# A graph network's second stage: other planned durations for its transfers, and one batch's attention put behind the last scores

## The chip, the cores and the metric

The kernel runs on one core of a Trainium2 chip, as one launch. The metric is the device time of that launch in microseconds. Three timed runs of the kernel before gave 3127.03, 3133.86 and 3125.08 us; their median, 3127.03 us, is what the changed kernel is compared with.

## The reference

Four graph layers follow each other on `x` (128 graphs of 128 nodes with 128 features, f32) and an adjacency `adj` (128 x 128 per graph, int32). Each layer adds its result to `x`. The change lies in the attention of the first one, whose core is this (`h` is the normalised, rectified `x`):

```python
D = jnp.abs(h[:, :, None, :] - h[:, None, :, :])        # 128 graphs, 128 x 128 pairs, 128 features
p = jnp.einsum('bijc,oc->bijo', D, W1) + b1             # 64 values per pair
p = (p - mean(p)) / jnp.sqrt(var(p) + EPS) * g1 + be1   # mean and variance over all graphs and pairs
s = jnp.einsum('bijo,uo->biju', leaky(p), W2)[..., 0] + b2[0]
A = softmax(jnp.where(adj > 0, s, NEG))
y = jnp.einsum('bij,bjc->bic', A, h) @ Wg.T + bg        # then normalised over all graphs
```

Two normalisations go over all 128 graphs. So all pair values have to exist before the first score, and all `y` before the second layer.

## The kernel before

The two normalisations cut the kernel into three stages. The first (to about 1253 us) makes the pair values of every graph. They are symmetric, so only half of them is kept: a tile `v` of 128 x 4064 f32 (2032 KB) per graph. Eight graphs' tiles stay in SBUF, those of the other 120 go to HBM (`pairs_d`). The second stage reads them back, makes scores, attention and `y`. The third runs everything else, four graphs at a time, and starts when `y` has been normalised.

The second stage takes the graphs in 16 batches of eight (`GS`). The batch that stayed in SBUF, number 15, comes first, then 0 to 14. So batch 14 is the last, and 13 the last but one. Its steps:

- `graph_scores` (L668 on): loads `v` of one graph (L677, on SP's DMA queue, into one of eight buffers); two halves of it get scale and bias on ACT (L657) and the leaky part on DVE (L428, at the end of `leaky`), the rest a rectifier on ACT (L664, tile `r`); then PE multiplies all with the weights (L702). The eight graphs of a batch gather in one PSUM tile `sc`. One graph's matmuls are called a score, or score group, below. When PE has finished a graph, its `v` buffer is free for the next load.
- `score_table`: after the eighth score, DVE adds a bias to the table (L721, tile `us`: the table step). Then POOL's DMA queue writes it to HBM in four pieces with the rows skewed (L731), and, when they have landed, reads it back (L742, tile `u`) in the layout that the symmetric matrix needs. Two tables in HBM are used in turn.
- `edges`, per four graphs: loads `adj` (L753, POOL's queue), makes the mask `negm` on DVE (L757) and squares the edges on ACT (L774) for the kernel's choice of third stage; loads `h` (L761, SP's queue, tile `ht`) and multiplies it with `Wg` (L765, tile `pz`, copied to `zg` at L768).
- `attention`, per four graphs, so twice per batch: an add on POOL (L784) completes `u`; PE sums the upper half, the transposed lower half and the mask (L791 to L794, tile `pl`: the logits); maximum and difference on DVE (L799, L801), exponential on ACT (L803), sum and division on DVE (L806 to L809), transposes on PE (L813), a copy on ACT (L816), the product with `zg` on PE (L820, tile `py`), the bias on ACT (L823), the store of `y` on POOL's queue (L825), and its statistics on DVE (L830, L831).
- `y_norm` takes the statistics of all graphs and gives scale and bias (`y_sc`, `y_bi`) to the third stage. `edge_types` (L849 to L857) makes the flag on which the program branches into the third stage.

The order of all this is not written out by hand. A planner, `in_order`, runs while the program is built. Each step is a generator that yields `(engine, planned duration, buffers taken, buffers freed)` before it emits its instructions. The planner starts up to ten chains at a time, gives each step a begin from when its engine, its predecessor and its buffers are free, and emits the step that can begin first; among equals, the older chain. `"wait", t` delays a chain in the plan by `t` us; `"after", name` holds a step until the plan has seen `"done", name`. Planned durations emit nothing. They only decide the order in which instructions stand on the engines, and each engine runs its instructions in that order. What really holds an instruction back on the chip are semaphores, which follow from the data and the buffers.

Of the kernel before, what the change touches and what calls it, by code (L numbers as in the profile page):

```python
# [24 lines left out]
GS = 8  # L25
GB = 4
# [20 lines left out]
PE, ACT, DVE, POOL, DMA = "PE", "ACT", "DVE", "POOL", "DMA"  # L47
# [115 lines left out]
def kernel(ctx: ExitStack, tc: tile.TileContext, x, adj, w, out):  # L163
    nc = tc.nc
    NB = x.shape[0]
# [267 lines left out]
    with tc.tile_pool(name="h_pool", bufs=1) as h_pool, tc.tile_pool(name="pairs", bufs=B_V) as b_v:  # L433
# [193 lines left out]
        with tc.tile_pool(name="b2", bufs=2) as b2p, tc.tile_pool(name="b_s", bufs=2, space=PSUM) as b_s, tc.tile_pool(  # L627
            name="b_ps", bufs=6, space=PSUM
        ) as b_ps:
            scores, masks = {}, {}  # L630
# [24 lines left out]
            def leaky_part(part, n):  # L655
                yield ACT, 0.2 + 0.00092 * n, "", ""
                nc.scalar.activation(part, part, AF.Identity, bias=h_bi, scale=h_sc)  # L657
                yield DVE, 0.15 + 0.00105 * n, "", ""
                leaky(nc.vector, part, part, 0.01)

            def relu_part(part, n, made):
                yield ACT, 1.1, "r", ""
                made["r"] = b2p.tile([P, 1024], F32, tag="r", name="r", bufs=B_R)
                nc.scalar.activation(  # L664
                    made["r"][:, 0:n], part, AF.Relu, bias=h_bi, scale=h_sc
                )

            def graph_scores(order, i):  # L668


                b = order[i]
                if b in here:
                    v = here.pop(b)
                else:
                    yield DMA, 5.2, "v", ""
                    v = b_v.tile([P, NPAIR], F32, tag="v", name="v")
                    nc.sync.dma_start(v, pairs_d[b])  # L677
                    yield "done", ("loaded", b)
                lin, made = first[NQ - 1], {}
                for a, e in ((0, lin // 2), (lin // 2, lin)):  # L680
                    yield "fork", leaky_part(v[:, a:e], e - a)
                yield "fork", relu_part(v[:, lin:NPAIR], NPAIR - lin, made)
                yield "join",
                r = made["r"]
                if i:
                    yield "after", ("w2", order[i - 1])
                yield PE, 3.2, "" if i else "sc", "v r"
                if i == 0:
                    scores[b // GS] = b_s.tile([P, 512], F32, tag="sc", name="sc")
                sc = scores[b // GS]  # L690
                for t in range(2):
                    k = b % GS + 2 * GS * t
                    begins, ends = i == t == 0, i == GS - 1 and t == 1
                    for q in [*range(NQ), NQ]:
                        rows = slice(QR * min(q, NQ - 1), QR * min(q, NQ - 1) + QR)
                        n = 8 * width[min(q, NQ - 1)]
                        if q < NQ:
                            z = v[:, first[q] + t * n : first[q] + t * n + n]
                        else:
                            z = r[:, t * n : t * n + n]  # L700
                        wz = w_slide if q < NQ - 1 else w_line if q < NQ else w_relu
                        nc.tensor.matmul(  # L702
                            sc[rows, 0:n], wz[:, 31 - k : 63 - k], z,
                            start=begins and q < NQ, stop=ends and q != NQ - 1,
                            tile_position=(0, rows.start),
                        )
                yield "done", ("w2", b)
                if i == GS - 1:
                    yield "done", ("scores", b // GS)

            def score_table(k):

                yield "after", ("scores", k)
                yield DVE, 1.6, "us", "sc"
                sc = scores.pop(k)
                sd = scores_d[k % 2]
                us = b2p.tile([P, 512], F32, tag="us", name="us")
                for s in range(2):
                    n = 8 * width[2 * s]
                    half = slice(64 * s, 64 * s + 64)  # L720
                    nc.vector.tensor_scalar(  # L721
                        us[half, 0:n], sc[half, 0:n], b2_rows[half, :], None, ALU.add
                    )
                yield POOL, 2.6, "u u", ""
                u = b2p.tile([P, GS, W], F32, tag="u", name="u")
                for q in range(NQ):
                    skewed = bass.AP(
                        tensor=sd.tensor, offset=sd.offset + QR * q * ROW + 1,
                        ap=[[W + 1, QR], [4 * ROW, 8], [1, width[q]]],
                    )  # L730
                    nc.gpsimd.dma_start(  # L731
                        skewed,
                        us[QR * q : QR * q + QR, 0 : 8 * width[q]].rearrange(
                            "p (r j) -> p r j", r=8
                        ),
                    )
                yield "wait", 3.0
                yield POOL, 1.2, "", "us"
                by_row = bass.AP(
                    tensor=sd.tensor, offset=sd.offset, ap=[[ROW - 1, P], [W + 1, GS], [1, W]]  # L740
                )
                nc.gpsimd.dma_start(u, by_row)  # L742
                yield "wait", 8.0
                for g in range(GS // GB):
                    yield "fork", attention(k * GS // GB + g, u[:, g * GB : g * GB + GB, :])
                yield "join",

            def edges(g):

                b0 = g * GB  # L750
                yield POOL, 0.7, "adj", ""
                adjs = b2p.tile([P, GB, P], I32, tag="adj", name="adj")
                nc.gpsimd.dma_start(adjs, adj_t[:, b0 : b0 + GB, :])  # L753
                yield "wait", 3.0
                yield DVE, 0.8, "negm", ""
                negm = b2p.tile([P, GB, P], F32, tag="negm", name="negm")
                nc.vector.tensor_scalar(negm, adjs, 0, NEG, ALU.is_le, ALU.mult)  # L757
                yield "fork", of_types(g, adjs)
                yield DMA, 0.6, "ht", ""
                ht = b2p.tile([P, GB, P], F32, tag="ht", name="ht")  # L760
                nc.sync.dma_start(ht, h_d[g])  # L761
                yield PE, 1.0, "pb", "ht"
                pz = b_ps.tile([P, GB, P], F32, tag="pb", name="pz")
                for i in range(GB):
                    nc.tensor.matmul(pz[:, i, :], ht[:, i, :], wgT, start=True, stop=True)  # L765
                yield ACT, 0.65, "zg", "pb"
                zg = b2p.tile([P, GB, P], F32, tag="zg", name="zg")
                nc.scalar.copy(zg, pz)  # L768
                masks[g] = negm, zg
                yield "done", ("edges", g)  # L770

            def of_types(g, adjs):
                yield ACT, 0.65, "", "adj"
                nc.scalar.activation(  # L774
                    adjs.bitcast(F32), adjs, AF.Square, bias=nhalf[:, 0:1], accum_out=squares[:, g : g + 1]
                )
                to_see.remove(g)
                if not to_see:
                    yield "done", "types"

            def attention(g, u):
                flat = "p g j -> p (g j)"
                yield POOL, 0.6, "", ""
                nc.gpsimd.tensor_tensor(  # L784
                    u[:, :, 0 : W - P], u[:, :, 0 : W - P], u[:, :, P:W], ALU.add
# [86 lines left out]
            ]  # L872
            makers = []

            for k in [NB // GS - 1, *range(NB // GS - 1)]:
                of_edges = [partial(edges, k * GS // GB + g) for g in range(GS // GB)]
                order = sorted(range(GS * k, GS * k + GS), key=lambda b: b not in here)
                of_graphs = [partial(graph_scores, order, i) for i in range(GS)]

                n = 0 if makers else 2  # L880
                makers += of_graphs[:n] + of_edges + of_graphs[n:] + [partial(score_table, k)]
# [484 lines left out]
def program(arrays):  # L1366

    import concourse.bacc as bacc

    nc = bacc.Bacc("TRN2", target_bir_lowering=False, num_devices=1)  # L1370
    ins, aps = {}, {}
    for name in ["x", "adj"] + _WEIGHTS:
        a = arrays[name]
        ins[f"in_{name}"] = a
        aps[name] = nc.dram_tensor(
            f"in_{name}", a.shape, mybir.dt.from_np(a.dtype), kind="ExternalInput"
        ).ap()
    out = nc.dram_tensor("out_0", arrays["x"].shape, F32, kind="ExternalOutput").ap()
    with tile.TileContext(nc) as tc:
        kernel(tc, aps["x"], aps["adj"], aps, out)  # L1380
    return nc, ins
# [10 lines left out]
```

## Time and profile before

| | us |
|---|---|
| median of three runs | 3127.03 |
| profiled execution, its own time | 3131.72 |
| its span, first to last instruction | 3129.9 |
| first score work of the second stage on ACT | 1253.3 |
| table step of batch 13 (DVE) | 1978.6 |
| table step of batch 14, the last | 2014.6 |
| last logits begin on PE | 2030.8 |
| `y_bi` done, third stage begins | 2052.0 |

The profile is one execution on the chip. "Busy" counts the time in which an engine has an instruction in work. A line of a timeline gives start and duration, then the engine, the source line, what is written from what, and in brackets how long the engine had been idle before and what ended that. The chain of waits follows the work that ended last back from the end: at each step to what released it, or else to the instruction ahead of it on its engine.

Shares of the whole span mix three stages with different limits. Over the span PE is busy 91%, DVE 85%, ACT 84%, POOL 48%. In the second stage, from 1400 to 1900 us, PE is busy 83 to 87 us of each 100, DVE 73 to 78, ACT 78 to 84, and the DMA engines move 383 to 407 GB/s.

These are the DMA issues of the second stage on the page (count, size of each, median time from issue to landing); the 240 of `v` are 120 stores of the first stage and 120 loads of the second:

```profile
v<-v SPq DMA_DIRECT2D x240, 2032.0 KB, 8.9
...
ht<-h SPq DMA_DIRECT2D x64, 256.0 KB, 6.3
u<-s POOLq DMA_DIRECT2D x16, 768.0 KB, 11.7
...
adj<-in_adj POOLq DMA_DIRECT2D x32, 256.0 KB, 7.5
y<-yt POOLq DMA_DIRECT2D x32, 256.0 KB, 6.2
```

### The profile page before, as it was taken

The numbers are of one execution on the slowest core, as the hardware profiler recorded it, in microseconds if no ns is written. First come the engines' busy times: TensorE is split into PE (matmuls) and PEld (weight loads), VectorE is DVE, ScalarE is ACT, GpSimd is POOL, SyncE is SP. The second block draws the span as 40 slices with busy tenths as digits, with TensorE's granted clock in tenths as the row PEclk, the third lists the DMA queues.
The fourth block names the chain that finished last, engine by engine and source line by source line (L and its number), as shares of the span: only waits on it lengthen the run. The fifth ranks groups of instructions, "written<-read, shape, count | busy, mean of one in ns | idle before, by whom it ended". The sixth has DMA issues, their size and how long they took to land. (4 is left out here: it accounts for less than half of the span.)

```text
span 3129.9 us, 47376 instructions
## 1 busy us (share of the span) xinstructions
PE 2852.8 (91%) x17526; PEld 1588.3 (51%) x17577; DVE 2656.4 (85%) x4730; ACT 2626.3 (84%) x3050; POOL 1494.6 (48%) x953
## 2 busy tenths in 40 slices
PE   6999999999999999787988888879999999999997
PEld 2444434333443333233333333367877777787776
DVE  6999999999999999776877877667787787787886
ACT  4999999999999998887877878657777877787786
POOL 5999999999999997111111111121222222222202
PEclk8999999999999999898999999989999999999999
DMA  3555555555555651899999999620111111111000
GB/s 120 241 239 240 242 239 244 227 227 244 236 227 228 252 224 41 351 393 381 402 405 406 397 409 400 227 75 11 45 48 35 48 38 45 41 38 42 18 1 22
DMA packets 150722, 606.53 MB, mean 194 GB/s; under 512 B 15633, under 2 KB 99026, under 8 KB 119762
## 3 DMA queue, kind: packets, MB, share of 16 engines
q1 hardware_dynamic: 140242, 569.86, 46.0%
q0 software_dynamic: 10240, 33.53, 3.0%
q8 instruction: 143, 2.34, 0.3%
q14 instruction: 97, 0.79, 0.1%
HBM read 322.74 MB, written 280.61 MB: 193 GB/s over the span
## 5 line engine op out<-in xcount | busy, mean ns | idle before, releaser
L552 POOL TENSOR_TENSOR d<-he 128x2016 f32<-128x2016 f32 (+1 forms) x288 | 1021.6, 3573 | 68.1 <-PE ph L569 62.2
L569 PE MATMUL ph<-d,w1T 128*64 128x512 f32 (+1 forms) x4096 | 927.5, 595 | 36.5 <-DVE d L549 17.6
L555 ACT ACTIVATE d<-d 128x2016 f32<-128x2016 f32 (+1 forms) x352 | 675.0, 1921 | 13.1 <-POOL d L552 13.0
L584 DVE BATCH_NORM_STATS2 six<-v 128x6 f32<-128x512 f32 (+1 forms) x1024 | 624.6, 670 | 5.6 <-ACT v L579 5.4
L569 PEld LDWEIGHTS ph<-d,w1T 128*64 128x64 f32 x4096 | 308.0, 136 | 546.2 <-issue 397.3
L579 ACT COPY v<-ph 128x1008 f32<-128x1008 f32 (+1 forms) x512 | 509.6, 1028 | 30.7 <-PE ph L569 27.9
L549 DVE TENSOR_TENSOR d<-he,pt 128x2048 f32<-128x2048 f32 (+1 forms) x224 | 505.5, 2257 | 2.6 <-PE ph L569 2.3
L939 POOL TENSOR_TENSOR rs<-ve,nhalf 128x4 f32<-128x4 f32 x96 | 119.1, 1241 | 738.6 <-DVE ve L936 480.4
L428 DVE SCALAR_TENSOR_TENSOR v<-v 128x1528 f32<-128x1528 f32 x256 | 434.0, 1742 | 34.2 <-ACT v L657 33.5
L657 ACT ACTIVATE v<-v,h_bi,h_sc 128x1528 f32<-128x1528 f32 x256 | 413.2, 1664 | 6.7 <-DVE h_bi L420 6.7
L702 PE MATMUL sc<-v,w_slide 128*32 128x512 f32 (+1 forms) x1536 | 322.6, 601 | 17.2 <-DVE v L428 16.9
L1095 PE MATMUL pa<-vals,p 128*128 128x99 f32 (+2 forms) x2048 | 253.2, 279 | 11.3 <-DVE p L966 7.7
L1095 PEld LDWEIGHTS pa<-vals,p 128*128 128x128 f32 x2048 | 248.5, 197 | 29.1 <-DVE p L966 11.3
L702 PE MATMUL sc<-v,w_line 128*32 128x504 f32 x512 | 261.0, 592 | 0.0
L702 PE MATMUL sc<-r,w_relu 128*32 128x504 f32 x512 | 259.1, 588 | 0.0
L966 DVE SCALAR_TENSOR_TENSOR p<-p,q 128x1024 f32<-128x1024 f32 (+1 forms) x192 | 206.7, 1083 | 48.5 <-ACT q L1082 24.4
L569 PE MATMUL ph<-both,us 128*64 128x512 bf16 x1920 | 236.4, 379 | 0.0
L569 PEld LDWEIGHTS <-us 128*64 128x64 bf16 x1920 | 124.4, 110 | 147.5 <-issue 91.6
L1081 ACT ACTIVATE p<-z 128x1024 f32<-128x1024 f32 x128 | 133.2, 1041 | 35.2 <-PE z L962 34.8
L664 ACT ACTIVATE r<-v,h_bi,h_sc 128x1008 f32<-128x1008 f32 x128 | 157.6, 1231 | 0.0
L702 PEld LDWEIGHTS sc<-v,w_slide 128*32 128x32 f32 x1536 | 65.1, 109 | 160.1 <-DVE v L428 83.3
L803 ACT ACTIVATE e<-e 128x512 f32<-128x512 f32 x32 | 20.2, 631 | 141.0 <-DVE e L801 141.0
(255 smaller groups left out, 4505.4 us busy)
## 6 DMA issues: line engine op xcount, KB each, us to landing
v<-v SPq DMA_DIRECT2D x240, 2032.0 KB, 8.9
xg<-in_x SPq DMA_DIRECT2D x64, 256.0 KB, 3.0
ht<-h SPq DMA_DIRECT2D x64, 256.0 KB, 6.3
u<-s POOLq DMA_DIRECT2D x16, 768.0 KB, 11.7
h<-he SPq DMA_DIRECT2D x32, 256.0 KB, 2.6
adj<-in_adj SPq DMA_DIRECT2D x32, 256.0 KB, 2.9
adj<-in_adj POOLq DMA_DIRECT2D x32, 256.0 KB, 7.5
y<-yt POOLq DMA_DIRECT2D x32, 256.0 KB, 6.2
```

The costliest lines, as they stand in the source:

```text
L428: engine.scalar_tensor_tensor(out, v, slope, v, ALU.mult, ALU.max)
L549: nc.vector.tensor_tensor(dv, later, own, ALU.max if larger else ALU.subtract)
L552: nc.gpsimd.tensor_tensor(dv, later, own, ALU.subtract)
L555: nc.scalar.activation(d[:, 0 : 4 * n], d[:, 0 : 4 * n], AF.Abs)
L569: nc.tensor.matmul(ph[64 * a : 64 * a + 64, t, 0:n], wt, x_, start=part == 0, stop=not larger or part == 3,)
L579: nc.scalar.copy(v.rearrange("p (t e) -> p t e", t=2), ph[:, :, 0:n])
L584: nc.vector.bn_stats(made["six"][:, 2 * q + t, :], v[:, t * n : t * n + n])
L657: nc.scalar.activation(part, part, AF.Identity, bias=h_bi, scale=h_sc)
L664: nc.scalar.activation(made["r"][:, 0:n], part, AF.Relu, bias=h_bi, scale=h_sc)
L702: nc.tensor.matmul(sc[rows, 0:n], wz[:, 31 - k : 63 - k], z, start=begins and q < NQ, stop=ends and q != NQ - 1, tile_position=(0, rows.st ...
L966: nc.vector.scalar_tensor_tensor(p, p, FLOOR, q, ALU.max, ALU.max)
L1095: nc.tensor.matmul(pa_all[:, h * (DH + 1) : h * (DH + 1) + n], p[:, h, :], vals_all[:, e : e + n], start=True, stop=True,)
```

## The change

Three planned durations get longer: the load of `v` from 5.2 to 5.8 us, the landing of the table's writes from 3.0 to 5.0, and the landing of `adj` from 3.0 to 8.0. None of them emits an instruction.

The order of the batches gets a name, `batches`, and `attention` is told its batch `k`. For the last batch but one (13), the planner holds the whole attention, from its add on POOL on, until it has planned the last score of the last batch (14). No instruction is added or taken away, and no tile or buffer changes.

```diff
-                    yield DMA, 5.2, "v", ""
+                    yield DMA, 5.8, "v", ""
...
-                yield "wait", 3.0
+                yield "wait", 5.0
                 yield POOL, 1.2, "", "us"
...
-                    yield "fork", attention(k * GS // GB + g, u[:, g * GB : g * GB + GB, :])
+                    yield "fork", attention(k, k * GS // GB + g, u[:, g * GB : g * GB + GB, :])
...
                 nc.gpsimd.dma_start(adjs, adj_t[:, b0 : b0 + GB, :])
-                yield "wait", 3.0
+                yield "wait", 8.0
                 yield DVE, 0.8, "negm", ""
...
-            def attention(g, u):
+            def attention(k, g, u):
                 flat = "p g j -> p (g j)"
+                if k in batches[-2:-1]:
+
+                    yield "after", ("scores", batches[-1])
                 yield POOL, 0.6, "", ""
...
-            for k in [NB // GS - 1, *range(NB // GS - 1)]:
+            batches = [NB // GS - 1, *range(NB // GS - 1)]
+            for k in batches:
```

## The prediction

> **What bounds the kernel now.** I read the slices of the page first. They show three stretches; the change touches only the middle one (about 1253 to 2052 us), where PE, ACT and DVE are all near 80% and the transfers near 100%. So I asked next for the windows of that stretch, then for who waits for whom in it, then for the chain through one batch of eight graphs, and last for the DMA queue of POOL.
>
> The slices of PE and DMA (40 of 78.2 us), one window of the stretch (columns: busy time and count of PE, PEld, DVE, ACT, POOL; TensorE clock; share of the DMA engines; GB/s), and the waits from 1340 to 1950 us:
>
> ```profile
> PE   6999999999999999787988888879999999999997
> ...
> DMA  3555555555555651899999999620111111111000
> ```
>
> ```profile
> 1600.00:1700.00 100.00, 85.89 (x476) 35.23 (x472) 77.65 (x84) 83.22 (x76) 14.52 (x22) 0.93 1.01 404
> ```
>
> ```profile
> POOL u L784 <- DMA u<-s: 130.7, 12, 13.5
> ACT e L803 <- DVE e L801: 106.4, 24, 11.9
> DVE mx L799 <- PE pl L794: 105.4, 24, 11.3
> PE pl L791 <- POOL u L784: 75.6, 12, 10.1
> ```
>
> The reader is to see that the DMA share is full, and yet that no line has an engine waiting for a load of `v`: PE, then DVE, then ACT all wait for `u`, the score table that comes back from HBM, once a batch. POOL's timeline through one batch and then the chain of waits (start, us, what) say what a batch's period is made of:
>
> ```profile
> 1833.86 2.36 POOL L731 DMA_DIRECT2D s<-us  x4 [7.52 <-DVE us L721]
> 1844.93 0.89 POOL L742 DMA_DIRECT2D u<-s  x1 [8.71 <-PE sc L702]
> 1856.11 1.40 POOL L784 TENSOR_TENSOR u<-u 128x256 f32<-128x256 f32 x2 [10.29 <-DMA u<-s]
> ...
> 1881.48 2.33 POOL L731 DMA_DIRECT2D s<-us  x4 [7.52 <-DVE us L721]
> ```
>
> ```profile
> 1856.88 2.08 PE pl L791 x2
> ...
> 1864.35 0.70 DVE mx L799
> ...
> 1868.98 0.63 PE pt L813 x4
> ...
> 1872.28 3.52 PE sc L702 x16
> ...
> 1876.89 3.53 PE sc L702 x20
> ```
>
> Period: 1881.48 - 1833.86 = 47.6 us. The table's DVE step starts 1.0 before its first write, at 1832.8, and the next one at 1880.4. From there to the logits (`pl`) at 1856.9 it is 24.1 us of two transfers in series (write 11.1, read 11.2); from the logits to the last score of the batch 23.5 us of PE work in its order. Their sum is the period. The read stands between "five score groups of the next batch" and "three score groups and the rest of the attention" in PE's order: what PE has in front of the logits is free while it fits into 24.1 us (it waited 5.3 at the end), what PE has behind them is paid in full.
>
> **What the Trainium skill says.** "DMA: Bandwidth & Descriptors", section "Queues, rings and completion order": each DMA engine takes turns between the queues that have work for it. The trace agrees: `u`, on POOL's queue, took 11.2 us here beside loads on SP's, and 5.4 (issued at 1989.6, its add at 1995.1) when none was left. So the two transfers shrink only when SP's queue is empty during them. "TensorE: Matmul & The Clock Gate", section "What's actually happening": an idle PE falls to half clock. It agrees: the first two `pl` matmuls took 2.08 us after the wait, the same pair of the second group 1.02. "Perfetto Trace Analysis", section "What "DMA-bound" means", looks for the bound in the DMA engines; here a share of 1.01 stands beside compute that never waits for them, so I follow the waits.
>
> **The change part by part.** Constants (5.2 to 5.8, 3.0 to 5.0, 3.0 to 8.0), the list `batches` and the argument `k` emit nothing; they decide the order. So I read the order of the two programs engine by engine. In before, every batch from the third attention on has on PE: 5 score groups, 2 logits, 1 score, 2 transposes, py, pz, py, score, pz, score. In after there are three patterns in turn, from the fourth attention on (four times A, four times B, three times C):
> A: 4 scores, logits, 2 scores, transpose, pz, py, transpose, score, py, pz, score.
> B: 4 scores, logits, score, 2 transposes, py, pz, py, 2 scores, pz, score.
> C: 5 scores, logits, score, transpose, pz, py, score, transpose, pz, py, score.
> The slower loads of the plan (5.8) let it think that four graphs fill the transfers. On the chip the loads are ahead, four groups take some 17 us (DVE does a half graph in 1.69: eight in 13.48), and PE waits sooner. The wait costs nothing new, but a score group (3.5) goes from the free side to the paid one.
>
> Walk from the logits, durations as above (logits 7.4 for the pair with half a clock, transpose 0.6, py 0.9, pz 1.1):
> A, PE: 7.4 + 3.5 + 3.5 + 0.6 + 1.1 + 0.9 + 0.6 + 3.5 + 0.9 + 1.1 + 3.5 = 26.6, with ACT's copies just inside it; I take 26.8, which is +3.3 on 23.5.
> B, DVE: second maximum at 7.5, its two steps 1.4, two sums 3.0, mask 0.35, two statistics 2.15, and eight half graphs before the table step, 13.5: 27.9, later than PE's 27.1; +4.3.
> C, PE: behind its second transpose stands ACT's copy at 19.9 (ACT does three half graphs, 1.6 each, and its other steps ahead of it), then py 0.9 and a score 3.5: 24.3, +0.8.
> The second and third attention move as C does, from 22.8 and 24.2: +1.6 together.
> Sum: 4 x 3.3 + 4 x 4.3 + 3 x 0.8 + 1.6 = 34.4 us. Do the 24.1 us shrink? Loads are issued as scores end. One score fewer stands before the wait, so SP's queue empties some 5 us sooner, at about 33 us after the table step instead of 38, still after `u` has landed at 23. I take no gain; bounds per batch are -2 (a quarter of the way to the 16.5 from the table step at 1978.6 to the add at 1995.1, when the loads ended) and +2: in A and C the store of `y`, on POOL's queue, is issued about 2 us before the table's writes instead of 7.5, and lies ahead of them.
>
> SP: one load of `ht` stands one place earlier among the loads of `v`; its buffer is free by then: 0. POOL: both loads of `adj` stand before both stores of `y`; the table's writes stay behind these: 0, else the +2 above.
>
> The moved attention (batch 13: 2 adds on POOL, 24 matmuls of logits, transposes and py and their loads, 2 x 5 steps of DVE, 2 x 3 of ACT, 2 stores). Before, it and two pz stood among the last eight scores: table step of batch 13 at 1978.6, of batch 14 at 2014.6, 36.0 us. After, the eight scores stand alone and ACT sets their pace: 6.5 graphs to do x 4.23 = 27.5, then 1.7 on DVE and 2.3 to 2.6 on PE: 31.5, a gain of 4.5. Then the moved work fills the wait for the last table. By the new order, from the last table step: logits to 5.7, pz 6.8, transpose 7.4, py 9.8, second transpose 11.0, py 12.8, its bias on ACT 13.5, its store 14.1; the last `u` took from 2014.6 to 2030.8 until its logits ran, 16.1. POOL's last add stands behind both stores, so the cover has 2 us left; without it each us of delay is a us of the end. Two things are late next: the flag for the branch is made some 7 us later (third-stage loads go out at about 10 us instead of 3; they are wanted at 37), which keeps them out of the way of `u`; and PE comes warm to the last logits. 37.3 us from table step to `y_bi` become about 35.2. Tail: -4.5 - 2.1 = -6.6.
>
> Sum against the profiled execution (3131.7 us, span 3129.9): +34.4 - 6.6 = +27.8, so about 3159.5; from the median of 3127.0, 4.7 lower: **3155 us**.
>
> **The rivals.** A run of this kernel is told from no change by about 0.3%, 9.4 us.
> 1. Forecast: the score moved behind the logits is paid. 0.64.
> 2. The transfers set the period: 47.7 us x 404 GB/s are 19.3 MB, and eight loads, the table and three small arrays sum to about that. Then `u` comes back sooner as the queue runs dry, the 34 us vanish and the tail remains: 3127 - 6.6 = 3120. For it: the share of 1.01. Against: no wait for a load; and at the early wait of 10.1 us, until 1376, the queue ran dry (171 GB/s from 1384 to 1388) only after `u` had landed. 0.17.
> 3. The change does what its constants say: PE's wait goes. Steady batches can't go below their transfers, so only the first ones (51.8, 50.9, 49.0) come down to 47.7, about -8, with the tail: 3112. Against: four scores before the logits, not six. 0.04.
> 4. As 1, with the stores of `y` delaying the table by 2 us in seven batches: +14, 3169 to 3172. It decides where a store is still running when the writes start. 0.15.
> Slower is then 0.64 + 0.15 = 0.79; rival 2 falls to 0.12 within and 0.05 below; faster 0.05 + 0.04 = 0.09. Range 3120 to 3176: the lower half of 2, and 3, are left out (about 0.12), and the top of 4 (0.07). The forecast's own range, by ±1.2 us a batch: 3140 to 3170.
>
> **What would show it.** Right: POOL's table writes about 51 us apart in A and B and 48.5 in C, PE waiting 8 to 10 us before the logits in A and B, transfers at 24 us, DMA share down to about 0.95, the last eight scores 31 to 32 us long. Wrong: a period of 47.7 with shorter transfers (rival 2), or logits that don't wait.

## The result, and the profile after

The changed kernel takes 3178.88 us (median of 4 runs, 3176.96 to 3190.89) against 3128.23 for the kernel before (4 runs, 3125.08 to 3133.86). The ratio is 1.0164, with a 95% interval of 1.0145 to 1.0182. It is slower, as forecast, but by 50.7 us and not by 28; 3178.9 lies above the range of 3120 to 3176. The profiled execution took 3179.55 us, its span 3177.8.

The slices of the page again (40 of 79.4 us), then one window of the second stage with the same columns as before the change:

```profile
PE   6999999999999998878787878879999999999997
...
DMA  3655655555555541999999999640111111111000
```

```profile
1600.00:1700.00 100.00, 75.42 (x401) 30.50 (x400) 66.05 (x72) 71.58 (x66) 13.27 (x20) 0.88 0.88 344
```

Every engine does less per 100 us, the DMA engines too: their share was 1.01 and is 0.88, at 344 GB/s instead of 404. Nothing became busier, so something is waited for longer. The waits from 1380 to 1990 us name it (total, times, longest):

```profile
POOL u L787 <- DMA u<-s: 146.5, 11, 13.7
DVE mx L802 <- PE pl L797: 143.8, 14, 13.3
ACT e L806 <- DVE e L804: 143.0, 14, 13.9
...
PE pl L794 <- POOL u L787: 106.9, 11, 11.3
```

It is the same wait as before, for the table `u` on its way back from HBM, but PE's part of it is now 9.7 us a time instead of 6.3. (All lines from the change on have moved by 3 to 4.) POOL's timeline through one batch of pattern A shows the period and the read:

```profile
1765.63 2.34 POOL L731 DMA_DIRECT2D s<-us  x4 [2.81 <-DVE us L721]
1776.07 0.90 POOL L742 DMA_DIRECT2D u<-s  x1 [8.09 <-PE sc L702]
1790.52 1.40 POOL L787 TENSOR_TENSOR u<-u 128x256 f32<-128x256 f32 x2 [13.55 <-DMA u<-s]
...
1816.16 0.56 POOL L828 DMA_DIRECT2D y<-yt  x1 [5.20 <-ACT yt L826]
1819.25 2.35 POOL L731 DMA_DIRECT2D s<-us  x4 [2.53 <-DVE us L721]
```

The period is 1819.25 - 1765.63 = 53.6 us; the forecast was about 51. From the issue of the read to the add on its result pass 1790.52 - 1776.07 = 14.5 us, where it was 11.2. The writes ahead of it, from the first write to the issue of the read, took 10.4 here and 11.1 before.

From the table step (DVE, L721), the first write (L731), the issue of the read (L742), its add (L787), the first logits (L794) and the next table step I summed the eleven middle batches, those from the fourth table step to that of batch 13:

| us, 11 batches | before | after | difference |
|---|---|---|---|
| first write to issue of the read | 125.1 | 117.6 | -7.5 |
| issue of the read to its add | 125.5 | 156.2 | +30.7 |
| table step to logits: these two, the step itself and the add | 270.6 | 293.9 | +23.3 |
| logits to the next table step | 258.4 | 297.1 | +38.7 |
| sum of the periods | 528.9 | 590.9 | +62.0 |

Ahead of these, the fourth table step comes at 1443.6 instead of 1449.7 (-6.1). Behind them, from the table step of batch 13 to `y_bi`, it is 67.0 us instead of 73.4 (-6.4). 62.0 - 6.1 - 6.4 = 49.5, and the spans differ by 47.9.

So the paid score cost 38.7 where 32.8 was forecast, and the way from table step to logits cost 23.3 where nothing was: the read 30.7 more, the writes ahead of it 7.5 less. What stood opposite the read can be seen on SP's queue. SP's timeline around one table step of before (at 1832.8), and then of after (at 1604.2):

```profile
1832.02 3.70 SPq L677 DMA_DIRECT2D v<-v  x2
1835.77 0.47 SPq L761 DMA_DIRECT2D ht<-h  x1
1840.65 0.32 SPq L677 DMA_DIRECT2D v<-v  x1
1841.02 0.44 SPq L761 DMA_DIRECT2D ht<-h  x1
1844.03 39.30 SPq L677 DMA_DIRECT2D v<-v  x7
```

```profile
1603.42 0.32 SPq L677 DMA_DIRECT2D v<-v  x1
1603.79 0.77 SPq L761 DMA_DIRECT2D ht<-h  x1
1606.81 0.32 SPq L677 DMA_DIRECT2D v<-v  x1
1607.17 0.54 SPq L761 DMA_DIRECT2D ht<-h  x1
1612.06 45.33 SPq L677 DMA_DIRECT2D v<-v  x7
```

In before, the two loads of `ht` go out 2.9 and 8.2 us after the table step, in after 0.4 before and 2.9 after it: about one load of `v` earlier. In the order of SP's queue both stand one load of `v` earlier in every middle batch. The DMA view of the stretch in which the data of one read is moved, first packet to last, of before (1849.2 to 1855.2) and of after (1780.2 to 1788.5), shows what that does (q1 is SP's queue, q0 POOL's; packets, MB, share of the 16 engines):

```profile
q1 hardware_dynamic: 229, 1.55, 65.5%
q0 software_dynamic: 188, 0.78, 35.5%
```

```profile
q1 hardware_dynamic: 198, 2.64, 79.3%
q0 software_dynamic: 174, 0.77, 23.3%
```

The same 0.77 MB of `u` came with 1.55 MB of SP's loads in 6.0 us before, and with 2.64 MB in 8.3 us after. In the trace's packet records a packet of `v` has 16,256 bytes and takes some 630 to 650 ns in the mean, one of `ht` 2,048 bytes and 90 to 100 ns, one of `u` mostly 4,608 bytes and 185 to 200. Per engine, ten of `u` stood in before beside 5.0 of `v` and 7.5 of `ht` (5.0 x 0.63 + 7.5 x 0.10 + 10 x 0.2 = 5.9 us), in after beside 10.1 of `v` and 0.9 of `ht` (10.1 x 0.65 + 0.9 x 0.09 + 10 x 0.19 = 8.5). In the mean of the eleven reads the 4.2 us from the issue to the first packet did not change; the data took 6.5 us before and 8.8 after, and 0.5 more passed between the last packet and the add. That is the reading; the experiments test it.

### The profile page after: what moved, and what is told of

The parts are those of the page before. It is cut to its first block, busy times and chain, and to the rows that moved or that the text cites. A ratio compares the mean times of both kernels' runs of the same rounds, so it can differ in the third digit from the quotient of the medians.

```text
span 3177.8 us, 47365 instructions
## 1 busy us (share of the span) xinstructions
PE 2853.8 (90%) x17526; PEld 1585.2 (50%) x17577; DVE 2658.3 (84%) x4730; ACT 2625.1 (83%) x3050; POOL 1495.3 (47%) x953
## 5 line engine op out<-in xcount | busy, mean ns | idle before, releaser
L428 DVE SCALAR_TENSOR_TENSOR v<-v 128x1528 f32<-128x1528 f32 x256 | 436.7, 1744 | 48.0 <-ACT v L657 46.6
L1099 PEld LDWEIGHTS pa<-vals,p 128*128 128x128 f32 x2048 | 247.8, 196 | 28.3 <-DVE p L970 11.2
L802 DVE TENSOR_REDUCE mx<-pl 128x4 f32<-128x512 f32 x32 | 22.0, 688 | 180.8 <-PE pl L797 180.8
L794 PE MATMUL pl<-u,ident 128*128 128x512 f32 x64 | 48.8, 855 | 133.0 <-POOL u L787 133.0
```

Of the source, the lines that this page charges most:

```text
L428: engine.scalar_tensor_tensor(out, v, slope, v, ALU.mult, ALU.max)
L1099: nc.tensor.matmul(pa_all[:, h * (DH + 1) : h * (DH + 1) + n], p[:, h, :], vals_all[:, e : e + n], start=True, stop=True,)
```

## The experiments

Each ratio is that of the experiment to the kernel before, with its 95% interval. The sums over eleven middle batches are made as above.

**One: the changed kernel, with `ht` put back by one load.** The issue of `ht` is held until the load of one more `v` has been issued, or until its reader comes; the order on the compute engines stays.

```diff
                     nc.sync.dma_start(v, pairs_d[b])
+                    to_load.discard(b)
+                    issue_held()
...
-                nc.sync.dma_start(ht, h_d[g])
+                held.append((ht, h_d[g]))
+                if not to_load:
+                    issue_held()
...
```

> The changed kernel, with each load of ht issued one place later on SP's queue, behind the next load of v, where the kernel before has it; the order on PE, ACT, DVE and POOL is that of the changed kernel. Theory P (place of ht): the read of u grew from about 11.4 to 14.2 us because POOL's queue and SP's take turns packet by packet, and only large packets of v stand opposite u when both ht are through; then the read is back at 11 to 12 us, from table step to logits it is 24 to 25 us instead of 26.6, and the kernel takes about 3179 - 11 x 2.3 = 3154 us (3148 to 3162). Theory R (the read is longer because fewer loads stand behind it, whatever the place of ht): read 14 us, 3179 us.

Measured: 3154.25 us (3142.50 to 3159.95), 1.0084 (1.0059 to 1.0110). The eleven reads sum to 125.5 us, as in before (after: 156.2), table step to logits to 268.2 (after: 293.9), logits to table step to 293.0 (after: 297.1). POOL's timeline of one batch of pattern A:

```profile
1600.35 2.34 POOL L739 DMA_DIRECT2D s<-us  x4 [2.81 <-DVE us L729]
1611.45 0.90 POOL L750 DMA_DIRECT2D u<-s  x1 [8.75 <-PE sc L704]
1621.91 1.40 POOL L798 TENSOR_TENSOR u<-u 128x256 f32<-128x256 f32 x2 [9.57 <-DMA u<-s]
...
1650.24 2.35 POOL L739 DMA_DIRECT2D s<-us  x4 [2.53 <-DVE us L729]
```

The read takes 10.5 us and the period is 49.9, with four scores ahead of the logits all the same. So about half of the loss, 24.6 us of 50.7 by the medians, is the place of `ht`. Without it the time is near the 3155 forecast, in part by luck: the walks behind the logits still cost 34.6, but the fourth table step came 4.9 us earlier than before, where 1.6 later was forecast, and the end saved 3.6 instead of 6.6.

**Two: the kernel before, with `ht` one load earlier.** The load of `v` is held instead, until the next `v` or `ht` is issued or its first reader comes.

```diff
-                    nc.sync.dma_start(v, pairs_d[b])
+                    issue_held()
+                    held.append((v, pairs_d[b]))
...
                 nc.sync.dma_start(ht, h_d[g])
+                issue_held()
...
```

> The kernel before, with each load of ht issued one place earlier on SP's queue, in front of the load of v that it followed, where the changed kernel has it; all else in the order of before. Theory P: read of u 13.5 to 14.5 us instead of 11.4, table step to logits 26 to 27 us, logits to the next table step unchanged at 23.5, so a batch takes about 50 us and the kernel 3128 + 12 x 2.3 = 3156 us (3148 to 3164). Theory R: nothing moves, 3128 us.

Measured: 3160.01 us (3158.34 to 3164.53), 1.0111 (1.0081 to 1.0140). Reads 158.5, table step to logits 295.5, logits to table step 266.7 (before: 258.4). One batch:

```profile
1649.08 2.33 POOL L742 DMA_DIRECT2D s<-us  x4 [7.52 <-DVE us L732]
1660.16 0.89 POOL L753 DMA_DIRECT2D u<-s  x1 [8.74 <-PE sc L707]
1674.31 1.40 POOL L796 TENSOR_TENSOR u<-u 128x256 f32<-128x256 f32 x2 [13.27 <-DMA u<-s]
...
1700.48 2.33 POOL L742 DMA_DIRECT2D s<-us  x4 [6.97 <-DVE us L732]
```

The read takes 14.2 us where PE's order has not been touched, and where POOL is idle for about 7 us before the table's writes, as in before. It is the place of `ht` alone; the stores, rival 4 of the prediction, have no part in it. I had expected the walk behind the logits to stay at 23.5 us; it took 24.2 in the mean. PE's two groups of logits took 8.1 us there and 7.35 in before, and that is the whole of the 8.3 us by which 266.7 exceeds 258.4. Why they are slower was not taken apart: in experiment four they took 7.9, after waits no longer than those of before.

**Three and four: the durations apart.** Three is the kernel before with only the 5.8; four is the changed kernel with 5.2 again, so with the two waits and the moved attention.

```diff
-                    yield DMA, 5.2, "v", ""
+                    yield DMA, 5.8, "v", ""
```

> The kernel before with one planned duration changed, the load of v from 5.2 to 5.8 us. PE then has four score groups ahead of the logits in every batch from the third attention on, and both loads of ht two places earlier. Theory A (one score group behind the logits is paid, and ht is through before the read): logits to table step 26.6 to 27.5 us, table step to logits 26 to 27, a batch about 53.5, the kernel 3128 + 12 x (3.1 + 2.3) = 3193 us (3183 to 3203), no gain at the end. Theory R (the two waits of the plan do it, not the load): near 3128 us.

> The changed kernel with the planned load of v back at 5.2 us; the two longer waits of the plan and the moved attention stay. PE has five score groups ahead of the logits again in every batch and ht stands where it stood before. Theory A: batches of 47.5 to 48 us as before, and the end from the table step of batch 13 to y_bi 67 us instead of 73.4: 3128 - 6.4 = 3122 us (3117 to 3127). Theory R (the waits of the plan cost something by themselves, since transposes stand one score later): 3130 to 3145 us.

Measured: three 3215.28 us (3209.38 to 3215.88), 1.0278 (1.0248 to 1.0309); four 3114.49 us (3103.67 to 3122.96, 20 runs), 0.9963 (0.9952 to 0.9973). Three does in every middle batch what the changed kernel does in eight of the eleven (A and B): four scores ahead of the logits. Its reads sum to 157.4, its logits to table step to 305.0, which is 46.6 above before. I had asked for too little: the eleven periods add 72.1 us, and the last eight scores, with the attention of batch 13 still among them, took 41.5 us instead of 36.0. Four is as fast in the middle as before (periods 525.7 against 528.9), with reads of 126.1. Its time lies below the 3117 to 3127 that I had given. So all of the loss comes from the 5.8, by both ways at once, and without it the rest of the change is a small gain. The parts do not add: beside the 5.8 the rest takes back 36 of the 87 us that three lost (3215.3 to 3178.9), 12 of them at the end and 10 in the eleven middle batches.

**Five: the moved attention alone.** The kernel before with the `"after"` of the change and its list of batches, and no other duration.

```diff
+                if k in batches[-2:-1]:
+                    yield "after", ("scores", batches[-1])
```

> The kernel before with nothing but the moved attention of batch 13; the three planned durations stay. Theory (the move saves at the end only, and the durations cost in every batch): 3128 - 6.4 = 3122 us (3118 to 3125); periods of the middle batches 47.5 to 48.2 as before, the last eight scores in about 31 us instead of 36.0. Rival (the move pays only together with the order that the durations make, since in the kernel before nothing is late there): 3128, no change.

Measured: 3118.93 us (3110.49 to 3125.30), 0.9970 (0.9954 to 0.9986). Middle periods 529.3, the last eight scores 31.4. It saves 7.8 by the medians. The interval overlaps that of four, so what the two waits add can't be told from nothing.

**Six: both loads of `ht` together, behind the later `v`.** On four; the issues wait for each other.

```diff
-                nc.sync.dma_start(ht, h_d[g])
+                held.append((ht, h_d[g]))
+                if len(held) == 2:
+                    issue_held()
...
```

> The changed kernel with the load of v planned at 5.2, and both loads of ht of a batch issued together behind the later v, so that all 512 KB of their small packets lie opposite the read of u. Theory (what stands opposite the read on SP's queue sets its length): the read falls from 11.4 to 9.5 to 10.3 us, the way from table step to logits by 1 to 2 us, and 12 batches give 12 to 20 us: 3098 (3092 to 3106) against 3114 for the same kernel with ht apart. Rival (the transfers as a whole set the period of 47.4 to 48.1, and a quicker read only moves the wait to the loads of v): the read is shorter but the period stays within 0.3 us, 3110 to 3118.

Measured: 3109.38 us (3106.96 to 3118.57), 0.9940 (0.9923 to 0.9956). During the data of a read 10 to 15 packets of `ht` per engine stood opposite, instead of 7.5, and the middle reads took 9.7 to 11.5 us, but for one of 13.6. But the interval overlaps that of four, and nine of the eleven periods stayed at 47.1 to 47.8; the profiled execution was also the slowest of the four. Inconclusive, and nearer the rival: at this period something else is close behind.

**Seven and eight: what the wait is worth, and the packets.** Seven covers the wait with scores instead of shortening it: on four, the landing of the writes is planned at 9.0 and that of the read at 13.0. In the trace seven score groups then stand between the table step and the logits of a middle batch, where four has five.

```diff
-                yield "wait", 5.0
+                yield "wait", 9.0
...
-                yield "wait", 8.0
+                yield "wait", 13.0
                 for g in range(GS // GB):
```

> The changed kernel with the load of v planned at 5.2, the landing of the table's writes at 9.0 and that of its read at 13.0: six scores between table step and logits instead of four, so seven before the logits. Theory (with four or five scores the chain through HBM ends last, and its cover is what counts): PE no longer waits for u, and what is late next is the transfers or PE itself; PE is busy about 41 us of a batch and the loads need about 47 at the 407 GB/s of before, so the period falls only to 46.5 to 47.5 and the time to 3105 (3095 to 3116). Rival (more scores ahead of the logits lengthen logits to table step, as the 5.8 does in the other direction, or hold the buffers of attention): 3120 to 3150.

Measured: 3093.55 us (3092.44 to 3100.27), 0.9897 (0.9880 to 0.9914), the fastest of all, and 1.5 us below the range I had given. A batch on POOL, the waits from 1460 to 1880 us and a window:

```profile
1574.32 0.91 POOL L742 DMA_DIRECT2D u<-s  x1 [6.95 <-PE sc L702]
1592.77 1.87 POOL L787 TENSOR_TENSOR u<-u 128x256 f32<-128x256 f32 x2 [17.54 <-DMA u<-s]
```

```profile
POOL u L787 <- DMA u<-s: 160.3, 9, 19.0
...
ACT v L657 <- DMA v<-v: 48.6, 36, 2.5
```

```profile
1600.00:1700.00 100.00, 87.72 (x482) 33.33 (x481) 80.45 (x90) 85.96 (x80) 17.64 (x22) 1.00 1.01 414
```

The read is the longest of all, 18.5 us, and PE doesn't wait for it: its wait for `u` is at most 0.3 us in eight of these nine batches, and its clock is 1.00. Its two groups of logits take 5.5 us, and in before, after the wait, 7.35 in the mean. Only `v` stands opposite this read. That alone doesn't make 18.5, since experiment nine has the same with 13.7 to 15.0; here some eight packets of 4,096 bytes per engine, of stores of `y` and a load of `adj` issued on POOL's queue behind the table's writes, move during the read as well. No run separates the two. What is late next is the load of `v`: ACT waits for it 36 times, at 414 GB/s. The period in these nine batches is 46.4 to 48.0, so the transfers' limit lay only some 1 us below the 47.7 of before. Most of the gain over before lies in the first batches: the fourth table step comes 27.4 us earlier than in before, the eleven middle batches take 15.0 less, and the end 4.6 more.

Eight takes the changed kernel and cuts each load of `v` into four, so that its rows are 4,064 bytes.

```diff
-                    nc.sync.dma_start(v, pairs_d[b])
+                    for c in range(0, NPAIR, NPAIR // 4):
+                        n = slice(c, c + NPAIR // 4)
+                        nc.sync.dma_start(v[:, n], pairs_d[b][:, n])
```

> The changed kernel, its durations and its order kept, with each load of v issued as four loads of a quarter of its columns (1016 of 4064 f32 per partition, so rows of 4 KB instead of 16 KB). Theory (what counts is the size of the packets that alternate with those of u): with packets of equal size opposite, the read of u needs 12 packets of its own and 12 of v per engine at about 170 ns, some 4 to 5 us and 2 us of latency: 6 to 9 us instead of 14; table step to logits falls to 18 to 21, PE's wait nearly goes, the periods fall by 5 to 8 us and the time to 3105 to 3140. Rival (the read is long because of the amount queued ahead of it or because ht itself delays it, not of the packets opposite): the read stays 13 to 15 us and the time at 3175 to 3185, or more if small packets carry v worse.

Measured: 3128.44 us (3124.07 to 3134.85), 1.0008 (1.0000 to 1.0017). The read on POOL, the DMA view while its data moves (1589.2 to 1593.0), and a window:

```profile
1585.14 0.90 POOL L744 DMA_DIRECT2D u<-s  x1 [6.54 <-DMA s<-us]
1594.13 1.41 POOL L789 TENSOR_TENSOR u<-u 128x256 f32<-128x256 f32 x2 [8.09 <-DMA u<-s]
```

```profile
q0 software_dynamic: 168, 0.76, 58.9%
q1 hardware_dynamic: 177, 0.64, 44.3%
```

```profile
1600.00:1700.00 100.00, 82.17 (x454) 31.53 (x453) 76.28 (x81) 81.62 (x74) 16.62 (x22) 0.97 1.03 394
```

The waits for `v` from 1460 to 1880 us:

```profile
ACT v L657 <- DMA v<-v: 61.9, 53, 3.3
```

The order is that of the changed kernel, and `ht` is through before the read; only the packets opposite are small. 0.76 MB of `u` now move in 3.8 us beside 0.64 MB of `v`, and the read takes 8.8 to 10.0 us instead of 14.2. The rival is out: it is the size of the packets opposite, not the amount queued. The read stayed longer than the 6 to 9 I expected because some 4 us pass between its issue and its first packet (1585.1 to 1589.2), here as in before and after; I had allowed 2, and 1.6 is what it takes in batch 13 of before and after, when no load stands opposite. The small packets have a price of their own: the DMA share is full at 394 GB/s, where the uncut loads of seven reach 414. ACT now waits for `v`, so the transfers set the period: the middle batches take 49.4 us in the mean, 1.3 more than in before, and it is the first batches (the fourth table step comes at 1428.5) that bring the time back to that of the kernel before.

**Nine: seven with the 5.8.** Six scores stand ahead of the logits in the middle batches.

```diff
-                    yield DMA, 5.2, "v", ""
+                    yield DMA, 5.8, "v", ""
```

> The changed kernel, load of v at 5.8 as in the change, with the landing of the table's writes planned at 9.0 and that of its read at 13.0: six scores before the logits in each batch instead of four or five, ht as early on SP's queue as in the changed kernel. Theory (the long read costs only what PE has no score to cover): the read stays at 14 us or longer and yet the time is 3095 to 3120, within 20 us of the same with 5.2. Rival (the 5.8 costs by something else as well, such as loads issued too late, so covering the chain doesn't bring it back): over 3130.

Measured: 3096.48 us (3090.17 to 3102.51), 0.9907 (0.9883 to 0.9931). The reads take 13.7 to 15.0 us and cost little, as PE waits 1.9 to 3.6 for them. The loads of `ht` are issued ahead of the read, but wait behind `v`: in one batch the read's packets move from 1582.8 to 1590.9 and those of `ht` from 1592.8 to 1603.1. So only `v` stands opposite here too. The 5.8 does no harm by itself. In the changed kernel it costs where it makes the planner put too few scores ahead of the logits and `ht` too early for them.

## Why the prediction was right or wrong

The direction was right and so was the mechanism that it named; the amount was wrong mainly by one step.

- **A score from the free side to the paid one.** Right. Logits to table step: A 26.6 to 27.1 us (forecast 26.8), C 24.1 to 24.2 (24.3). B took 29.0 to 29.5 instead of 27.9, and DVE ends it, as forecast: in the walk from 1524.7 PE's last score is done at 1552.2, and the table step comes 1.5 us later, behind a half graph of `v` for which DVE had waited 0.8 us on ACT. The pair of logits took 8.0 us there, not 7.4, so the second maximum came at 8.1 and not at 7.5. (27.9 less 23.5 is 4.4, not the 4.3 of the forecast.) The four B together make 5.5 of the 5.9 us by which 38.7 exceeds the forecast's 32.8. With `ht` put back (experiment one) the eleven walks cost 34.6.

```profile
1532.80 0.69 DVE L802 TENSOR_REDUCE mx<-pl 128x4 f32<-128x512 f32 x1 [0.86 <-PE pl L797]
...
1544.61 6.66 DVE L428 SCALAR_TENSOR_TENSOR v<-v 128x1528 f32<-128x1528 f32 x4
1552.06 1.75 DVE L428 SCALAR_TENSOR_TENSOR v<-v 128x1528 f32<-128x1528 f32 x1 [0.79 <-ACT v L657]
1553.73 1.52 DVE L721 TENSOR_SCALAR us<-sc,b_rows 64x512 f32<-64x512 f32 x2
```

- **"SP: one load of `ht` stands one place earlier among the loads of `v`; its buffer is free by then: 0."** This is the step that failed. Both loads of `ht` stand one place earlier, and it is not 0. I asked whether `ht` could be issued, and not what it stood opposite to. Its place decides what the read of `u` alternates with, and through "I take no gain; bounds per batch are -2 ... and +2" the 24.1 us from table step to logits went into the sum unchanged. They measured 26.7 in the mean, 2.1 a batch above before. Experiment one gives back 24.6 us by it; experiment two, with no other order changed, loses 34.4 by the medians of its comparison. In its eleven middle batches the reads take 33.0 more and the writes ahead of them 8.1 less, so 24.9 from table step to logits, and the walks behind the logits take 8.3 more. The prediction had the needed sentence in hand. The Trainium skill, "DMA: Bandwidth & Descriptors", section "Queues, rings and completion order", has the engines take turns between queues by whole packets; I drew from it only that a second queue slows the read, and that it shrinks only when SP's queue is empty; experiment eight, with loads on SP's queue all the while and their packets small, has it at 8.8 to 10.0. The size of the second queue's packets says by how much it is slowed. The packet counts agree with taking turns at 1 to 1.7 for one: 10 to 17 data packets per engine opposite ten of `u` in the middle batches of before, after and experiments seven and eight, whether they have 2, 4 or 16 KB. A packet of the page holds several descriptors, a packet record of the trace here one row; that the two are the same no run shows.
- **The bound of +2 had the wrong cause.** The 2.1 measured lies just above it, but it stood for the stores of `y`. They do stand closer to the table's writes in A (3.1 us, in the timeline above), yet the writes took less time than before, 10.7 in the mean against 11.4. Rival 4 had a time near the result and is refuted all the same.
- **Rival 2, the transfers set the period.** Wrong for this kernel: with periods of 50 to 56 us the DMA share fell to 0.88 in the window shown. Its arithmetic was right, and it takes over as soon as the wait is covered or short: in experiments seven and eight ACT waits for `v`.
- **First batches.** Forecast +1.6 for the second and third attention; in fact the fourth table step came 6.1 earlier. The cause stays open. Experiments three and five, which have the old waits, had it at 1450.7 and 1451.4, and four, which has the new ones, at 1439.9; but two, with the old waits and the order of before, had it at 1444.4. And five, whose order up to there is that of before, had its first table step at 1303.5 where before had 1296.7, so single executions differ by as much as is to be explained.
- **Tail.** Right in sum: the last eight scores took 30.8 us (forecast 31.5) and the rest up to `y_bi` 36.2 (35.2), so table step of batch 13 to `y_bi` fell by 6.4 (6.6). In experiment five, which has the move alone, it fell by 9.5.

By terms, from the profiled execution: forecast 32.8 + 1.6 + 0 - 6.6 = 27.8; measured 38.7 - 6.1 + 23.3 - 6.4 = 49.5.

## What to carry to other kernels

When an edit shifts a transfer on one queue, look up which latency-bound transfer of another queue it stood opposite, and count packets by size there: here the waiting transfer's data took the time of its own packets plus 1 to 1.7 times as many of the other queue's. Where a round trip through HBM holds the tensor engine once per batch, count the work that stands ahead of the wait before shortening it: on experiment four, two more scores ahead gave 21 us, a shorter read 5, which is not clear of the noise. A planner's duration is a lever on order and not a measurement: the planned load that is nearer to the 6.0 us per load of the traced period (47.7 us for eight) gave the slower order, and with the longer waits of experiment nine it cost nothing that could be told.

## What the runs showed of the hardware

- The same 768 KB read on POOL's queue took, from issue to the add on its result, 5.1 to 6.1 us with no loads opposite (batch 13 of before, after and experiments one to six), 8.8 to 10.0 beside 4 KB packets (eight), 11.4 in the mean beside a mix of 2 KB and 16 KB (before), 14.2 beside mostly 16 KB (after), 13.7 to 15.0 beside 16 KB alone (nine), and 18.4 to 19.9 where transfers of its own queue moved in between as well (seven). Before its first packet pass 1.6 us with no loads opposite (batch 13 of before and after), about 4 in the middle batches of before, after, eight and nine, and 4.4 to 8.6 in seven.
- Loads in packets of 16,256 bytes ran at 414 GB/s with a DMA share of 1.01 (seven), the same loads in packets of 4,064 bytes at 394 with 1.03 (eight).
- PE's two groups of logits took 5.5 us in seven, where it hardly waited for them, and 7.35 in the mean in before, where it waited 5.1 to 7.2 us.
- A DMA share of 1.01 stood beside a kernel (before) that was within about 1 us per batch of the transfers' limit and yet waited on latency: seven, with the wait covered, took 1% less at the same share. Part of that 1% is the moved attention; the cover alone, from four to seven, is 0.7%.
